# The first attention block begins with its own four units, and layer 0's last tokens begin at the second unit

## The chip, the cores and the metric

The kernel runs on one core of a Trainium2 chip. The core has five engines that take their instructions in order and wait for each other through semaphores: TensorE (PE in the profile; its weight loads are PEld), VectorE (DVE), ScalarE (ACT), GpSimd (POOL) and SyncE (SP), whose queue issues most DMA transfers. The metric is the device time of one execution in microseconds (us), lower is better. The change is judged by the median of several runs.

## The reference

Four images of 128 channels and 64 x 64 pixels go through two layers. Layer 0 normalises by groups of channels, makes three 1x1 convolutions and attends over the 4096 pixels; its result is added to the input. Layer 1 takes the pixels as tokens of 128 channels: an attention of 16 heads with 8 channels each, a small feed-forward part, and a recurrence over the tokens. The change lies in layer 1's attention, cut here to what matters.

```python
def _L1_attn_ref(x, rx_theta, ...):
    heads = x.reshape(Bs, Ss, H, D)                 # H = 16 heads, D = 8
    qkv = _qz_ring(heads + rx_theta)                # products of cosines
    q = jnp.transpose(qkv, (0, 2, 1, 3))
    scores = jnp.einsum('bhsd,bhtd->bhst', q, q) / np.sqrt(D)
    attn = jax.nn.softmax(scores, axis=-1)
    ctx = jnp.einsum('bhst,bhtd->bhsd', attn, q)
    ...
```

Queries, keys and values are the same `q`. The matrix of scores is therefore symmetric, and the kernel computes only about half of it: the exponentials of a tile serve its rows, and, transposed, its columns.

## The kernel before

**Stages.** An image n goes through `first_stage` (layer 0, and its tokens in 8 chunks of 512), `second_stage` (layer 1's attention) and later, between the steps of the next image, its feed-forward part. The tokens of a chunk are made by the generator `tokens` (line 674), in some 15 steps between `yield`s: statistics (line 717), `normalise` (721), the cosines in `cos_steps` (224), products (746 to 751), a transposition (759) and two transfers into `parts_dram` (767). The last chunk is not finished in layer 0: its generator is handed to `attention` (line 769) as `tail`, and one step of it runs in each unit there (line 1198), from the third unit on. When it has ended, `rest` (853) loads the last quarter of keys and queries. Until then no unit may use tokens of the last quarter (line 1118).

**Units.** The 16 heads are taken as 8 pairs. For a pair the 4096 queries are cut into 4 blocks (`NQB`) of 1024 (`QB`), and the keys into 32 tiles of 128. A unit is one turn of the loop at line 1117: two tiles of keys against the block's queries. Its work:

- TensorE: scores into PSUM (line 1125, four matmuls in four parts of the array).
- ScalarE: two exponentials of 128 x 1024 (line 1137). Their place is chosen by `exps` (1089): a pool of six tiles, or, in two of five turns, parts of the image's tile `xs`, which layer 0 no longer needs (while `tail` lives, only the first of the two).
- TensorE, two units later: `weigh` (929) adds the weighted values into `acc`, a PSUM tile with one buffer (`ps_acc=(ONE, 1)`), new in each block.
- When a block's last unit has been weighed, `finish` (968) has VectorE transpose `acc` into `o` (line 972), GpSimd copy `o` (980), and later steps gather the rest.

**Own units and the others.** The order of a block's units comes from `order` (1066). Four of them are the block's own: both tiles lie in the block's own 1024 tokens, and nothing of them serves another block (`off` is false at line 1120). The other units, `off`, serve a second block too: ScalarE also sums their exponentials (`accum_out`), VectorE transposes them ("flips", line 900, in `run_flips`), and TensorE then makes mirror steps (line 913): a group of four off units gives 16 steps, each of four matmuls. They add up in one of two slots of the PSUM tile `misc`, and VectorE adds the sum into `later` (927). Blocks 0 and 1 of a pair have 16 off units and 4 own ones, blocks 2 and 3 have 12 and 4. In most blocks the own units stand between the others, one after each four (each three); only in the very last block of an image they come last.

**What sets the order.** The engines' order around attention is written out by hand (`tc.manual_schedule`, line 1747): TensorE, ScalarE, VectorE and GpSimd take instructions as the Python code issues them. SP's transfers are placed by the scheduler. Three rules meter the mirror work:

- A unit adds to `credit` 3.3 steps (3.15 from block 2 on) if it is off, and 3.0 if it is own, up to 4.75 and 8.25 (lines 1150 to 1156). `run_pending` (875) takes that many whole steps, of one group only. A group is available two turns after its fourth flip (line 902).
- `run_flips` (891) issues the flips of at most two units a turn (line 1196).
- It holds the flips of a group while the group two before it has steps left, because a group's flipped tiles are used again:

```python
                if g >= 2 and groups[g - 2]["steps"]:
                    return
```

**Loads.** `prepare` (807) asks for a pair's keys and queries, one tile for each block, from pools of six tiles each. In pair 0 the first loads are those that the first unit needs (lines 845 to 850); the last block's wait for `rest`. The scratch tiles of `tail` come from the same pools.

Of the kernel before, what the change touches and what calls it, by code (L numbers as in the profile page):

```python
# [26 lines left out]
def kernel(  # L27
# [42 lines left out]
    NQB = S // QB  # L70
# [41 lines left out]
    def get(kind, name):  # L112
        if callable(here[kind]):
            return here[kind](name)
        pool, shape = here[kind]
        return pool.tile(shape, F32, tag=kind, name=name)
# [652 lines left out]
    def attention(n, q, xs, tail, upcoming):  # L769
# [12 lines left out]
        fixed, _ = here["fixed"]  # L782
# [24 lines left out]
        def prepare(pair):  # L807

            own = qb[:, :, ts(pair, 2 * D)].rearrange("p (k a) (h d) -> p a k h d", a=4, d=D)
            qa = q_aug[pair % 2]  # L810
            qv = qa[:, 0 : NT * 2 * V].rearrange("p (k s h e) -> p s k h e", s=4, h=2, e=V)

            def copy_q(k0, k1):
                for a in range(4):
                    for s in range(4):
                        nc.gpsimd.tensor_copy(  # L816
                            qv[ts(a, 32), s, k0:k1, :, 0:D], own[ts(s, 32), a, k0:k1]
                        )

            keys = [get("keys", f"keys{n}_{pair}_{b}") for b in range(NQB)]
            queries = [get("queries", f"queries{n}_{pair}_{b}") for b in range(NQB)]
            def load_queries(b):
                for h in range(2):
                    for x in range(2):
                        for y in range(2):
                            row = ((2 * pair + h) * 2 + y) * D
                            src = parts_dram[row : row + D, ts(2 * b + x, IC)]
                            nc.sync.dma_start(  # L830
                                out=queries[b][ds(64 * h + 32 * x + 16 * y, 16), :],
                                in_=src.unsqueeze(0).broadcast_to([2, D, IC]),
                            )

            def load_keys(b):
                for h in range(2):
                    row = (2 * pair + h) * 2 * D
                    src = parts_dram[row : row + 2 * D, ts(b, QB)]
                    nc.sync.dma_start(
                        out=keys[b][ts(h, 64), :], in_=src.unsqueeze(0).broadcast_to([4, 2 * D, QB])  # L840
                    )


            there = NQB if pair else NQB - 1
            load_keys(1)
            load_queries(0)
            for b in [0] + list(range(2, there)):
                load_keys(b)
            for b in range(1, there):
                load_queries(b)  # L850
            copy_q(0, NTG if pair else NTG - 1)

            def rest():
                if pair == 0:
                    copy_q(NTG - 1, NTG)
                    load_keys(NQB - 1)
                    load_queries(NQB - 1)

            later = get("later", f"later{n}_{pair}")
            nc.gpsimd.memset(later, 0.0)  # L860
            denom = get("denom", f"denom{n}_{pair}")
            return (keys, queries, qa, later, denom), rest
# [28 lines left out]
        def run_flips(most):  # L891
            while most and flips:
                g, k, es = flips[0]
                if g >= 2 and groups[g - 2]["steps"]:
                    return
                group = groups[g]
                if k == 0:
                    group["e"] = [get("flipped", f"t{group['name']}_{h}") for h in range(2)]
                for h in range(2):
                    nc.vector.transpose(group["e"][h][:, k, :], es[h])  # L900
                if k == TG - 1:
                    pending.append((turn + 2, group["steps"], group["block"]))
                flips.pop(0)
                most -= 1
# [158 lines left out]
            else:  # L1063
                late.extend([mirrored, result])

        def order(b, own_last):


            own = [(QT * b + k, QT * b + TG + k) for k in range(TG)]
            halves = [(v, v) for v in range(2 * b + 2, 2 * b + (5 if b < NQB // 2 else 4))]  # L1070
            halves.insert(2, (2 * b + 1, 2 * b + (5 if b < NQB // 2 else 4)))
            rest = [
                tuple(v % (2 * NQB) * TG + k for v in vs) for vs in halves for k in range(TG)
            ]
            if own_last:
                return rest + own
            each = len(rest) // TG
            return [u for k in range(TG) for u in rest[each * k : each * (k + 1)] + own[k : k + 1]]

# [9 lines left out]
        def exps(name, last):  # L1089


            k = turn % 5 - 3
            if k < 0 or last or (k and tail):
                return [get("exps", f"e{name}_{h}") for h in range(2)]
            return [xs[:, ts(2 * k + h, QB)] for h in range(2)]

        waiting = []
        turn = 0
# [4 lines left out]
        ends, late = [], []  # L1103
        fixed_tiles()
        ready, rest = prepare(0)
        w = mirror_weights(0, 0)
        for pair in range(NPAIR):
            keys, queries, qa, later, denom = ready
            for b in range(NQB):
                block = {"acc": None}  # L1110
                end_of_all = pair == NPAIR - 1 and b == NQB - 1
                tiles = order(b, end_of_all)

                coming = (pair, b + 1) if b < NQB - 1 else (pair + 1, 0)
                if coming[0] == NPAIR:
                    coming = None
                for at, unit in enumerate(tiles):
# [4 lines left out]
                    for h in range(2):  # L1122
                        for x in range(2):
# [6 lines left out]
                                stop=True,  # L1130
                            )
                    es = exps(name, end_of_all)

                    split = off and unit[0] != unit[1]
# [38 lines left out]
                    if at == 6 and b == 1 and pair + 1 < NPAIR:  # L1173
                        upcoming_pair = prepare(pair + 1)[0]
# [20 lines left out]

                    if at:
                        run_flips(2)
                    if tail and turn > 2 and next(tail, tail) is tail:
                        tail = None
                        rest()  # L1200
                    if end_of_all and at in (0, len(tiles) - 1):
# [509 lines left out]
    def second_stage(im, tail, upcoming):  # L1711
# [33 lines left out]
        with stage(f"attn{n}", sides, others, ("queries", "keys"), **pools):  # L1745
            engines = {e.engine for e in (nc.tensor, nc.scalar, nc.vector, nc.gpsimd)}
            with tc.manual_schedule(engines=engines):
                im["left"] = attention(n, im["q"], im["xs"], tail, upcoming)
# [109 lines left out]
    for n in range(N):  # L1858
# [5 lines left out]
        tail = first_stage(image, before)  # L1864
# [153 lines left out]
    with tc.If(any_bad > 0):  # L2018
# [5 lines left out]
        with stage(  # L2024
# [8 lines left out]
            pool, _ = here["big"]  # L2033
# [95 lines left out]
```

## Time and profile before

| | us |
|---|---|
| median of 3 runs | 6939.8 (6939.42 to 6941.01) |
| the profiled execution, its own time | 6941.1 |
| its span, first to last instruction | 6939.0 |
| mean granted TensorE clock | 0.992 |
| attention of image 0: first scores, first scores of pair 1, of pair 2, of pair 3 | 397.8, 560.7, 715.0, 869.3 |
| the same of image 1 | 2096.7, 2258.5, 2412.8, 2567.1 |
| the same of image 2 | 3794.8, 3955.2, 4109.6, 4263.9 |
| the same of image 3 | 5494.2, 5654.8, 5809.1, 5963.4 |
| half clock of TensorE in image 0's first block | 400.9 to 407.7, and 428.2 to 431.6 |
| in image 1's | 2100.7 to 2107.6, and 2124.6 to 2131.4 |
| in image 2's | 3797.2 to 3804.0, and 3824.5 to 3827.9 |
| in image 3's | 5497.0 to 5503.8, and 5524.3 to 5527.7 |

The first part of the profile's page lists each engine's busy time, its share of the span and its instructions. Later rows are groups of instructions: line, engine, operation, what is written and read, count, busy time, mean duration in ns, and idle time of the engine just before them, with what ended it. In a timeline a row begins with its start and length in us. A wait is put down to the instruction that ended it. The granted clock is a share of full speed; outside the stretches above it is 1.0 in the attention of pairs 0 to 3.

### The profile page before, as it was taken

Reading aid. Unit: us, or ns where it says so; the run is one execution under the profiler, and the core shown is the slowest. Engines: PE = TensorE matmul, PEld = TensorE weight load, DVE = VectorE, ACT = ScalarE, POOL = GpSimd, SP = SyncE. Lnnn points to the kernel's source line nnn. Section 1 sums busy time; section 2 is a strip of 40 time slices with the busy share of each in tenths; the row PEclk is TensorE's granted clock in tenths of the full one; section 3 lists DMA queues with packets and bytes.
Section 4 is the critical chain, followed back from the end, with each engine's and each line's share of the span. In section 5 each row is a group of like instructions: output and inputs, shape, how many; then the busy total and the mean of one; then the engine's idle time right before and its main releaser. Section 6 shows DMA issues by size and latency. Waiting matters only on the chain. (4 is left out here: it accounts for less than half of the span.)

```text
span 6939.0 us, 223539 instructions
## 1 busy us (share of the span) xinstructions
PE 6806.3 (98%) x92343; PEld 3652.9 (53%) x92343; DVE 5971.1 (86%) x8073; ACT 5931.6 (85%) x11841; POOL 2775.2 (40%) x10008
## 2 busy tenths in 40 slices
PE   9999999999999999999999999999999999999997
PEld 5545555555664555555565455555566555555554
DVE  6688988897888899889788999888978898889888
ACT  4479999997668999999676999999956699999985
POOL 1134444444333444444433344444443343444443
PEclk9999999999999999999999999999999999999998
DMA  1110000000111000000011100000001100000013
GB/s 33 40 39 30 27 31 21 22 10 23 46 53 44 31 24 25 21 22 9 31 50 52 40 25 24 25 21 24 18 28 49 51 31 21 22 24 24 20 54 119
DMA packets 88792, 226.17 MB, mean 33 GB/s; under 512 B 9832, under 2 KB 10736, under 8 KB 86992
## 3 DMA queue, kind: packets, MB, share of 16 engines
q1 hardware_dynamic: 85772, 206.39, 8.8%
q8 instruction: 726, 11.89, 0.7%
q10 hardware_dynamic: 1732, 5.24, 0.2%
q14 instruction: 306, 2.51, 0.1%
q0 software_dynamic: 256, 0.13, 0.0%
HBM read 147.73 MB, written 56.62 MB: 29 GB/s over the span
## 5 line engine op out<-in xcount | busy, mean ns | idle before, releaser
L1137 ACT ACTIVATE e<-s 128x1024 f32<-128x1024 f32 (+1 forms) x3480 | 2949.8, 902 | 94.0 <-PE s L1125 71.5
L900 DVE STREAM_TRANSPOSE t<-e 128x1024 f32<-128x1024 f32 x2240 | 2593.4, 1210 | 63.2 <-ACT e L1137 60.2
L913 PEld LDWEIGHTS misc<-t,mirror 128*32 128x32 f32 x57344 | 1654.8, 110 | 1327.8 <-issue 1278.8
L913 PE MATMUL misc<-t,mirror 128*32 128x128 f32 x57344 | 1967.6, 273 | 20.2 <-DVE later L927 14.3
L1137 ACT ACTIVATE xs<-s 128x1024 f32<-128x1024 f32 (+1 forms) x2152 | 1838.7, 908 | 58.8 <-PE s L1125 46.1
L900 DVE STREAM_TRANSPOSE t<-xs 128x1024 f32<-128x1024 f32 x1344 | 1562.6, 1210 | 37.7 <-ACT xs L1137 36.2
L934 PE MATMUL acc<-e,q_aug 128*32 128x512 f32 x11360 | 1522.7, 608 | 1.2 <-POOL q_aug L816 1.2
L1125 PE MATMUL s<-queries,keys 32*128 32x512 f32 x9216 | 1240.4, 496 | 9.6 <-ACT e L1137 5.7
L980 POOL COPY own<-o 32x36 f32<-32x36 f32 x2048 | 432.2, 211 | 1838.4 <-DVE o L972 1758.5
L934 PE MATMUL acc<-xs,q_aug 128*32 128x512 f32 x7072 | 942.2, 605 | 0.0
L573 ACT ACTIVATE p<-s 128x1024 f32<-128x1024 f32 x512 | 500.4, 1022 | 412.3 <-PE s L569 408.2
L1125 PEld LDWEIGHTS s<-queries,keys 32*128 32x128 f32 x9216 | 485.4, 182 | 587.3 <-issue 293.3
L580 PE MATMUL acc<-p,asmT 128*128 128x512 f32 x1536 | 707.7, 595 | 0.0
L1137 ACT ACTIVATION_READ_ACCUMULATOR e<-s 128x1 f32 x2880 | 696.0, 242 | 0.0
L1005 POOL COPY other<-turned 32x64 f32<-32x64 f32 x1904 | 444.4, 233 | 620.2 <-DVE turned L995 541.7
L870 POOL COPY mirror<-q 32x128 f32<-32x128 f32 x2048 | 596.2, 291 | 188.7 <-PE misc L913 100.6
L594 DVE TENSOR_TENSOR total<-total,p 128x1024 f32<-128x1024 f32 x448 | 548.4, 1224 | 23.5 <-ACT p L573 15.6
L569 PE MATMUL s<-hl,e 128*128 128x512 f32 x1536 | 442.1, 429 | 5.7 <-ACT p L573 4.7
L580 PEld LDWEIGHTS acc<-p,asmT 128*128 128x128 f32 x1536 | 287.8, 190 | 262.0 <-issue 245.2
L966 POOL COPY by_token<-by_key 32x4 f32<-32x4 f32 x2000 | 387.6, 194 | 84.4
L1137 ACT ACTIVATION_READ_ACCUMULATOR xs<-s 128x1 f32 x1728 | 420.7, 243 | 0.0
L934 PEld LDWEIGHTS acc<-e,q_aug 128*32 128x32 f32 x11360 | 225.5, 108 | 351.8 <-issue 349.9
(355 smaller groups left out, 5066.8 us busy)
## 6 DMA issues: line engine op xcount, KB each, us to landing
keys<-parts_dram SPq DMA_DIRECT2D x256, 256.0 KB
queries<-parts_dram SPq DMA_DIRECT2D x1024, 32.0 KB
x_dram<-x SPq DMA_DIRECT2D x56, 256.0 KB
fx<-x_dram SPq DMA_DIRECT2D x48, 256.0 KB
t_dram<-t2T SPq DMA_DIRECT2D x32, 256.0 KB
t2s<-t_dram SPq DMA_DIRECT2D x16, 512.0 KB
hl<-hl SPq DMA_DIRECT2D x28, 256.0 KB
parts_dram<-high SPq DMA_DIRECT2D x28, 256.0 KB
```

The lines of the kernel that those rows point to most:

```text
L569: nc.tensor.matmul(s[:, j, :], stationary, moving, start=y == 0, stop=y == len(parts) - 1)
L573: nc.scalar.activation(p, s, AF.Exp)
L580: nc.tensor.matmul(state["acc", ic], values_at(tile_of(2 * jp + j)), p[:, j, :], start=jp == 0 and j == 0, stop=jp == NP - 1 and j == 1,)
L594: nc.vector.tensor_tensor(state[ic], state[ic], p, ALU.add)
L870: nc.gpsimd.tensor_copy(wv[ts(a, 32), s, :, :, ts(a, D)], own[ts(s, 32)])
L900: nc.vector.transpose(group["e"][h][:, k, :], es[h])
L913: nc.tensor.matmul(state["acc"][ts(2 * x + h, 32), :], state["w"][:, QT * (s // 4) + TG * x + s % 4, h, :], state["e"][h][:, :, ds(IC * x ...
L934: nc.tensor.matmul(it["in"]["acc"][ts(2 * h + x, 32), :], it["qa"][:, ds((2 * it["tiles"][x] + h) * V, 32)], it["e"][h][:, ts(x, IC)], sta ...
L980: nc.gpsimd.tensor_copy(own[ts(s, 32), ts(x, 4), h, :], ov[ts(2 * h + x, 32), s, :, 0:V])
L1005: copy(to[ts(k, 32), h], tv[ts(2 * x + h, 32), k])
L1125: nc.tensor.matmul(ss[h][:, x, :], keys[unit[x] // QT].bitcast(F32R)[r, ts(unit[x] % QT, P)], queries[b].bitcast(F32R)[r, :], start=True, ...
L1137: nc.scalar.activation(es[h][:, ts(x, IC)] if split else es[h], ss[h][:, x, :] if split else ss[h].rearrange("p x c -> p (x c)"), AF.Exp, ...
```

## The change

Four edits, all in `attention`:

1. `order` gets an argument `own_first`. In block 0 of pair 0 of each image the four own units come first, and then the other 16 without interruption.
2. `tail` begins at the second unit (`turn > 1`) and no longer at the third.
3. In pair 0 the tile of keys of block 1 is taken from the pool ahead of that of block 0, and the keys of block 0 are loaded first, since the first unit now reads them.
4. While `tail` lives, `exps` doesn't use `xs` in the first five turns.

```diff
-            keys = [get("keys", f"keys{n}_{pair}_{b}") for b in range(NQB)]
+            keys = {b: get("keys", f"keys{n}_{pair}_{b}") for b in ((0, 1, 2, 3) if pair else (1, 0, 2, 3))}
...
-            load_keys(1)
+            load_keys(1 if pair else 0)
             load_queries(0)
-            for b in [0] + list(range(2, there)):
+            for b in [0 if pair else 1] + list(range(2, there)):
                 load_keys(b)
...
-        def order(b, own_last):
+        def order(b, own_last, own_first):
...
-            if own_last:
-                return rest + own
+            if own_last or own_first:
+                return own + rest if own_first else rest + own
...
-            if k < 0 or last or (k and tail):
+            if k < 0 or last or (tail and (k or turn < 5)):
                 return [get("exps", f"e{name}_{h}") for h in range(2)]
...
-                tiles = order(b, end_of_all)
+                tiles = order(b, end_of_all, pair == b == 0)
...
-                    if tail and turn > 2 and next(tail, tail) is tail:
+                    if tail and turn > 1 and next(tail, tail) is tail:
                         tail = None
                         rest()
```

The computation, the number of instructions on each engine and the rules for `credit`, `run_flips` and `run_pending` are the same. The lines of the two kernels have the same numbers.

## The prediction

> **What bounds the kernel now.** I read the page first, then TensorE's and VectorE's timelines around the first attention block, the windows with the granted clock, and last the view of line 972, because the change delays the work that surrounds it.
>
> ```profile
> PE 6806.3 (98%) x92343; PEld 3652.9 (53%) x92343; DVE 5971.1 (86%) x8073; ACT 5931.6 (85%) x11841; POOL 2775.2 (40%) x10008
> ...
> L900 DVE STREAM_TRANSPOSE t<-e 128x1024 f32<-128x1024 f32 x2240 | 2593.4, 1210 | 63.2 <-ACT e L1137 60.2
> ```
> TensorE is busy 98% of the span; VectorE has 14% spare over the whole, and a flip (line 900) is its costliest work.
>
> ```profile
> 453.80 0.50 PE L1125 MATMUL s<-queries,keys 32*128 32x512 f32 x4
> 454.24 1.06 PE L934 MATMUL acc<-e,q_aug 128*32 128x512 f32 x8
> 455.12 1.06 PE L913 MATMUL misc<-t,mirror 128*32 128x128 f32 x32
> 456.11 0.50 PE L1125 MATMUL s<-queries,keys 32*128 32x512 f32 x4
> ```
> One unit on TensorE, by distances between starts: scores 0.44, weighing 0.88, four mirror steps 0.99 (0.25 each). A unit lasts 2.31 us with four steps, 2.08 with three.
>
> ```profile
> 422.69 1.06 PE L934 MATMUL acc<-e,q_aug 128*32 128x512 f32 x8
> 427.94 1.75 PE L913 MATMUL misc<-t,mirror 128*32 128x128 f32 x32 [4.19 <-DVE later L927]
> ...
> 422.00:428.00 6.00, 1.81 (x28) 0.46 (x24) 6.00 (x8) 5.50 (x16) 0.00 (x0) 1.00 0.00 0
> 428.00:432.00 4.00, 4.00 (x52) 2.09 (x56) 4.00 (x4) 1.77 (x3) 2.43 (x6) 0.57 0.00 0
> 450.00:470.00 20.00, 20.00 (x352) 10.14 (x352) 17.47 (x19) 19.24 (x36) 13.53 (x49) 1.00 0.24 90
> ```
> (The last three lines: stretch, length, busy time of TensorE, its weight loads, VectorE, ScalarE, GpSimd, each with its instructions, granted clock, DMA share, GB/s.) Image 0, 25 us into attention: VectorE, full with flips and layer 0's last tokens (6.00 of 6), is late; TensorE waits 4.19 us and then works at 0.57 of its clock. The four images' such waits sum to 14.3 us. From 450 on TensorE never stops.
>
> ```profile
> L972 DVE STREAM_TRANSPOSE o<-acc x128: 707/717/718, 453.1 to 6739.3; 128x512 f32<-128x512 f32 x128
> ...
>   PE acc L934: 132.3, 125
> who waited for it (us, times):
>   POOL own L980: 1758.5, 100
>   PEld acc L934: 0.3, 1
> ```
> At the end of a block VectorE transposes the sum `acc` out of its only PSUM buffer. 125 times of 128 VectorE sat waiting for TensorE; TensorE waited for it once, 0.3 us. This margin is what the change spends.
>
> **Own units first: the mirror work starts four units later.** An own unit makes no flip and no mirror step. Counted from 0, units 0 to 3 were off-diagonal; their group of 16 steps was released two turns after the fourth, at unit 6. Now units 4 to 7 are the first group, and its steps begin at unit 10. Steps run in the pattern 4, 4, 3, 3, 2 a group, so by the end of the 20-unit block the old order has done 46 of 64 (units 6 to 19), the new one 32 (units 10 to 19): 14 steps behind. No work is added, but catching up is slow. The credits pay 3.3 steps an off unit (3.15 from block 2 on) and 3.0 an own: 64.8 in blocks 0 and 1, 49.8 in blocks 2 and 3, against 64 and 48 needed, a surplus of 2(0.8 + 1.8) = 5.2 a pair. 14 / 5.2 = 2.7 pairs.
>
> **Where the lag bites.** Line 894 holds the flips of group g until group g-2 has no steps left. In the old block 0, group (8,8) has its last step in unit 10, just as the first unit two groups on asks for its flip: nothing is held. In the new one that last step falls in unit 14, and the asking units are 12 to 15. From block 1 on a whole group is held and then released in two turns: 8 transposes back to back. By VectorE's rows six starts cover 6.8 us, so 1.13 each and 9.0 for eight, in some 4.2 us of TensorE's time.
>
> I replayed both built orders with this trace's numbers: each engine takes its instructions in order, one starts when its engine's slot is over and what it waits for has ended; slots are median distances between starts. The old order, replayed, puts pair 3 469 to 471 us after each image's attention start; the trace has 471.5, 470.4, 469.1 and 469.2. So I trust the replay inside attention to a few us an image.
>
> One stall, worked out. Pair 0, unit 54: group g-2 ends and eight flips start, with line 972 behind them: 9.0 + 0.72 = 9.7 us until `acc` is free. TensorE asks for the new block's `acc` at unit 58, after three units (6.2) and one set of scores (0.5): 6.7 us. It stands 3.0 us; the replay says 3.1. Queued behind that weighing are the mirror steps that would free the next flips, and all later scores. The trace of before shows no such wait beyond 0.3 us. Bounds for one: 0 (VectorE's spare time takes it) and 7.1 (release one turn ahead: 9.7 less 2.6). For the block ends of the lag the replay gives 0.4, 3.1, 2.8, 3.6, 2.7, 0.7, 1.3, 1.5, 0.7: 17 us an image, nearer the lower end, and I take it.
>
> **The sum.** TensorE's idle time in the first four pairs, old to new in the replay: 10 to 31 us in image 0, 8 to 24 in the others: +70 in all. This already contains what the change cures: in images 1 to 3 the old wait of 3.2 to 3.5 us shrinks to 0.7 and block 1 begins some 3 us earlier. In image 0 it is not cured: GpSimd still copies mirror weights (line 870) until 410, so the tail's reciprocal root (line 221, ended at 411.2) comes no earlier, normalising stands on it, and behind that now every flip; the held exps stop ScalarE.
>
> Next, 57 more sets of scores begin in halves, since the second half waits for an exp that waits for a late flip. The four matmuls of a set overlap, and a split costs up to another 0.43: at most 24, the replay has 21.
>
> Last, the clock. The old trace grants half clock after stretches that were 0.4 to 0.7 busy; image 1's wait of 3.2 us cost 6.8 us of it. The replay, halving below 0.58 busy, has 61 us more at half clock: 31 us lost. Halving below 0.50 gives 22, below 0.66 53. I take 31, since 0.58 lies between what the trace shows.
>
> The Trainium skill ("TensorE: Matmul & The Clock Gate", Part 1) says that TensorE falls to half clock only after an idle window of about 3.4 us; by that rule hardly a stall of 2.7 to 3.6 us would cool it, and the sum would be some 91 instead of 122. The trace's 3.2 us wait did cool it, so I keep the row.
>
> 70 + 21 + 31 = 122. The profiled execution took 6941.1 (span 6939.0 and 2.1 around it), 1.3 above the median 6939.8, which lies between runs of 6939.42 and 6941.01; so 6939.8 + 122 = **about 7062 us, slower by 1.8%.** I say 7060.
>
> **The edits costed at nothing.** Starting the tail one turn earlier puts VectorE's tokens ahead of the flips (inside the replay). Unit 3's exps move from `xs` to the pool: its six tiles hold three units, and unit 0's are free once weighed, since nothing flips them. Keys: block 0's and block 1's halves are issued tens of us before attention in both orders; without that cover the first scores would wait a landing, of which the nearest row is 1.84 us for a 256 KB write. On SP's queue nine of pair 1's query loads (three before) now pass the last keys of pair 0, and the ninth waits for block 0's queries until unit 19. Those keys are wanted at unit 30, eleven units or 23 us later; without that cover TensorE would stand some 2 us an image. GpSimd's queue keeps its order, but the next block's mirror copies now wait for a lagging group (5.3 us of copies, a 42 us block to hide in).
>
> **Rivals.** *The start is cured and the lag is free* (VectorE's spare time absorbs the bursts; for it: 426 us busy of 473 in the first three pairs of image 1, against it: bursts do not wait for an average). Then the 14.3 us of waits go and about half of 17 us at half clock, 8.5; four more units without steps, idle 0.7 us each (2.0 for two exps by ScalarE's starts, 400.76 and 401.75, less 1.3), give back 11 over four images: 6939.8 - 23 + 11, about 6928. Chance 0.04. *A wash*: the lag catches up within pair 0, so only the first three or so of the waits arise, some 3 us an image after the gain of 3: 6935 to 6952. Chance 0.03. *The lag is worse*: each of the four long stalls costs two windows of half clock as image 1's did, and ScalarE starves for free exps: half-clock cost 53 or more, 7085 to 7120. Chance 0.13. *No effect*, since the order would be rebuilt by a scheduler: against it, the built order shows own units first on TensorE, ScalarE and VectorE.
>
> **How the numbers follow.** Forecast 0.80: 7060, its own range 7025 to 7085. The range of 8 in 10 takes in part of the worse case and a replay that counts half of the idle time: 7020 to 7095. A change under 0.2% (14 us) could not be told from none; faster 0.04, same 0.03, slower 0.93.
>
> **What would show it.** Right: in the changed profile line 934 on TensorE waits for line 972, some nine times over 0.3 us an image, all in pairs 0 to 2; half clock then; pairs 3 to 7 as long as before; the wait on line 927 gone in images 1 to 3. Wrong: no wait on line 972, or pair 3 beginning within 5 us of its old distance from the start (I expect 25 to 37 more). If the first block of images 1 to 3 is not about 3 us shorter, the start was misread.

## The result, and the profile after

| | before | after |
|---|---|---|
| median of 5 runs beside each other, us | 6941.01 (6939.42 to 6944.32) | 7066.35 (7063.72 to 7066.51) |
| span of the profiled execution | 6939.0 | 7064.6 |
| TensorE busy | 6806.3 | 6856.1 |
| TensorE at half clock, all stretches added | 120.1 | 167.5 |

The changed kernel is slower: ratio 1.018, 95% interval 1.0169 to 1.0191. The forecast was 7060, in a range from 7020 to 7095.

The first part of the page of after, and four of its rows (the columns are those of before):

```profile
PE 6856.1 (97%) x92343; PEld 3678.3 (52%) x92343; DVE 5965.9 (84%) x8073; ACT 5947.4 (84%) x11841; POOL 2774.2 (39%) x10008
...
L900 DVE STREAM_TRANSPOSE t<-e 128x1024 f32<-128x1024 f32 x2240 | 2588.6, 1208 | 43.2 <-ACT e L1137 41.2
L913 PE MATMUL misc<-t,mirror 128*32 128x128 f32 x57344 | 1984.3, 274 | 10.6 <-DVE t L900 5.8
...
L934 PE MATMUL acc<-e,q_aug 128*32 128x512 f32 x11392 | 1535.4, 611 | 53.4 <-DVE o L972 52.1
...
L934 PE MATMUL acc<-xs,q_aug 128*32 128x512 f32 x7040 | 942.3, 607 | 19.8 <-DVE o L972 19.8
```

Every engine has as many instructions as before, and a flip costs the same 1.21 us. The new thing stands at the end of the two rows of line 934: 52.1 and 19.8 us of idle time, ended by line 972. Before, the same two rows had 1.2 and 0.0 us of idle time, none of it from line 972:

```profile
L934 PE MATMUL acc<-e,q_aug 128*32 128x512 f32 x11360 | 1522.7, 608 | 1.2 <-POOL q_aug L816 1.2
...
L934 PE MATMUL acc<-xs,q_aug 128*32 128x512 f32 x7072 | 942.2, 605 | 0.0
```

TensorE's waits in after, longest sums first (what waited, for what: us in all, times, longest one):

```profile
PE acc L934 <- DVE o L972: 71.9, 36, 3.7
PE s L1125 <- ACT e L1137: 18.3, 30, 1.7
...
PE misc L913 <- DVE t L900: 5.8, 5, 3.3
```

Before, the second of these was 5.7 us in 12 waits, and another one stood there, which is gone:

```profile
PE misc L913 <- DVE later L927: 14.3, 4, 4.2
```

Line 972 itself, in the view that lists who waited for it:

```profile
  PE acc L934: 79.8, 75
...
who waited for it (us, times):
...
  PEld acc L934: 90.9, 60
  PE acc L934: 71.9, 36
```

The first line is VectorE's side: it now sat waiting for TensorE 75 times, where it had done so 125 times of 128. The last line is TensorE's side: 36 waits, 2.0 us each, nine in each of the four images, where before there was one of 0.3 us that held only the weight load.

One of them at close range, the first weighing of block 3 of pair 0 in image 0. First VectorE's timeline in after:

```profile
532.43 4.62 DVE L900 STREAM_TRANSPOSE t<-e 128x1024 f32<-128x1024 f32 x4
536.97 4.58 DVE L900 STREAM_TRANSPOSE t<-xs 128x1024 f32<-128x1024 f32 x4
541.47 0.67 DVE L972 STREAM_TRANSPOSE o<-acc 128x512 f32<-128x512 f32 x1
```

and TensorE's timeline beside it:

```profile
538.60 0.50 PE L1125 MATMUL s<-queries,keys 32*128 32x512 f32 x4
542.20 1.06 PE L934 MATMUL acc<-e,q_aug 128*32 128x512 f32 x8 [3.10 <-DVE o L972]
543.09 1.12 PE L913 MATMUL misc<-t,mirror 128*32 128x128 f32 x24
544.14 0.80 PE L1125 MATMUL s<-queries,keys 32*128 32x512 f32 x4
```

Eight flips run back to back from 532.43 to 541.55 and the small transposition of `acc` stands behind them, 0.67 us long. TensorE has nothing left at 539.10 and waits until 542.20. From 543.5 on its instructions are longer (a set of scores 0.80 instead of 0.50). That is the clock, as the windows of the same stretch show (stretch, length, busy time and instructions of TensorE, granted clock, DMA share, GB/s):

```profile
536.66:540.07 3.41, 2.44 (x40) 1.00 0.26 84
540.07:543.49 3.42, 1.29 (x24) 1.00 0.15 57
543.49:546.90 3.41, 3.41 (x36) 0.50 0.11 43
```

The wait of 3.10 us is followed by 3.41 us at half clock: some 1.7 us more are lost.

### The profile page after: what moved, and what is told of

Same layout as the page of the kernel before. It is cut to its first block, busy times and chain, and to the rows that moved or that the text cites. A ratio compares the mean times of both kernels' runs of the same rounds, so it can differ in the third digit from the quotient of the medians.

```text
span 7064.6 us, 223521 instructions
## 1 busy us (share of the span) xinstructions
PE 6856.1 (97%) x92343; PEld 3678.3 (52%) x92343; DVE 5965.9 (84%) x8073; ACT 5947.4 (84%) x11841; POOL 2774.2 (39%) x10008
## 5 line engine op out<-in xcount | busy, mean ns | idle before, releaser
L934 PE MATMUL acc<-e,q_aug 128*32 128x512 f32 x11392 | 1535.4, 611 | 53.4 <-DVE o L972 52.1
L900 DVE STREAM_TRANSPOSE t<-xs 128x1024 f32<-128x1024 f32 x1344 | 1558.9, 1208 | 16.6 <-ACT xs L1137 15.1
L1125 PE MATMUL s<-queries,keys 32*128 32x512 f32 x9216 | 1268.7, 498 | 24.4 <-ACT e L1137 18.3
L934 PE MATMUL acc<-xs,q_aug 128*32 128x512 f32 x7040 | 942.3, 607 | 19.8 <-DVE o L972 19.8
L1125 PEld LDWEIGHTS s<-queries,keys 32*128 32x128 f32 x9216 | 500.8, 182 | 585.7 <-issue 320.1
L1137 ACT ACTIVATION_READ_ACCUMULATOR e<-s 128x1 f32 x2880 | 680.4, 236 | 0.0
L927 DVE TENSOR_TENSOR later<-later,misc 128x128 f32<-128x128 f32 (+1 forms) x576 | 162.1, 281 | 460.1 <-PE misc L913 456.0
```

Source lines behind the costliest of these rows:

```text
L934: nc.tensor.matmul(it["in"]["acc"][ts(2 * h + x, 32), :], it["qa"][:, ds((2 * it["tiles"][x] + h) * V, 32)], it["e"][h][:, ts(x, IC)], sta ...
L1125: nc.tensor.matmul(ss[h][:, x, :], keys[unit[x] // QT].bitcast(F32R)[r, ts(unit[x] % QT, P)], queries[b].bitcast(F32R)[r, :], start=True, ...
L1137: nc.scalar.activation(es[h][:, ts(x, IC)] if split else es[h], ss[h][:, x, :] if split else ss[h].rearrange("p x c -> p (x c)"), AF.Exp, ...
```

## The experiments

All changes of time are against runs of the kernel before, taken on the same chip beside those of the changed one. The waits are those of the matmuls, from the profiled execution; waits of a weight load alone aren't counted. "Shift of pair 3" is by how much later than before pair 3 begins, counted from the image's attention start, summed over the four images. Half clock is TensorE's time at half clock, in the whole profiled execution and in pairs 0 to 2 of the four images (before: 120.1 and 44.4). Outside these pairs it varies from 62 to 99 us with no visible relation to the waits, so the column of pairs 0 to 2 is the one to compare.

| kernel | time, us | ratio (95%) | change | waits of line 934 for 972 | half clock | of it in pairs 0 to 2 | shift of pair 3 |
|---|---|---|---|---|---|---|---|
| after | 7066.35 | 1.0169 to 1.0191 | +125 | 71.9 | 167.5 | 88.7 | +128 |
| order_alone | 7078.55 | 1.0176 to 1.0210 | +133 | 72.1 | 174.6 | 99.0 | +134 |
| rest_alone | 6943.64 | 0.9987 to 1.0006 | -2 | none | 146.9 | 47.8 | +1 |
| old_late_steps | 7084.29 | 1.0183 to 1.0217 | +139 | 70.0 | 188.2 | 116.1 | +148 |
| catch_up | 6954.28 | 1.0004 to 1.0023 | +9 | none | 119.5 | 37.5 | +13 |
| one_own_first | 6947.99 | 0.9998 to 1.0016 | +5 | none | 130.1 | 44.4 | +6 |
| two_own_first | 6951.07 | 1.0003 to 1.0022 | +8 | 6.6 | 133.2 | 44.4 | +8 |
| three_own_first | 7001.79 | 1.0075 to 1.0108 | +59 | 43.3 | 133.5 | 71.7 | +62 |
| two_own_faster_start | 6951.69 | 1.0003 to 1.0021 | +9 | 5.3 | 125.0 | 47.8 | +7 |
| acc_copied | 7006.57 | 1.0077 to 1.0111 | +64 | copy instead | 121.6 | 37.5 | +61 |
| acc_copied_old | 7008.92 | 1.0079 to 1.0113 | +66 | copy instead | 124.9 | 41.0 | +54 |

The kernel before had medians of 6945.32, 6942.88 and 6942.89 beside the three groups of experiments. The last column agrees with the change of time to within 12 us everywhere: what a kernel loses, it loses in the first three pairs of each image.

### Which of the four edits it is

**order_alone**: the kernel before with the first edit only.

```diff
-                tiles = order(b, end_of_all)
+                tiles = order(b, end_of_all, pair == b == 0)
...
+            if own_last or own_first:
+                return own + rest if own_first else rest + own
```

> The old kernel with the own units first in block 0 of pair 0 and nothing else of the change (tail from the third unit, keys, queries and exps as before). Lag theory: the order alone makes the mirror steps late, so nearly all of the cost is here: +110 to +140 us over before, line 934 waits for line 972 some 36 times, 60 to 75 us in sum. Rival 'the moved tail, the exchanged keys or the exps edit cost the time': within 15 us of before.

Measured +133, with the same waits as after. From TensorE's waits of this kernel:

```profile
PE acc L934 <- DVE o L972: 72.1, 37, 3.7
```

**rest_alone**: the other three edits on the old order.

```diff
-                tiles = order(b, end_of_all)
+                tiles = order(b, end_of_all, False)
...
-            if k < 0 or last or (k and tail):
+            if k < 0 or last or (tail and (k or turn < 5)):
...
-                    if tail and turn > 2 and next(tail, tail) is tail:
+                    if tail and turn > 1 and next(tail, tail) is tail:
```

> The changed kernel with the old order of units, so the other three edits alone. Lag theory: no lag, no wait on line 972; -10 to +5 us against before, with the 14 us of waits on line 927 nearly as before. Rival 'the other edits cost it': +60 us or more.

Measured no change (-2), and the old wait of line 913 for line 927 is still there, 12.8 us in all. So the order of the units carries the whole loss. The other edits cost nothing by themselves. With the new order it is +125 with them and +133 without, but the intervals of the two ratios overlap, so that they take some of its cost away isn't shown.

### Whether it is the lag of the mirror steps

**old_late_steps**: the kernel before with its old order, where only the first group's steps are released four turns later. No unit moves.

```diff
-                    pending.append((turn + 2, group["steps"], group["block"]))
+                    pending.append((turn + (6 if g == 0 else 2), group["steps"], group["block"]))
```

> The old kernel and the old order of units; only the first group of 16 mirror steps of each image is released six units after its last flip and not two, which makes the same lag of four units without any other order. Lag theory: +110 to +150 us, waits of line 934 on line 972 of 55 to 75 us, all in pairs 0 to 2. Rival 'sixteen off-diagonal units in a row overload VectorE and ScalarE in the first block': the order is the old one, so at most the four units' missing steps, 0 to +15 us.

Measured +139. This is the clearest of the runs: the order of the units is the old one, and the lag alone brings the waits and the loss. From TensorE's waits of this kernel:

```profile
PE acc L934 <- DVE o L972: 70.0, 33, 3.7
PE s L1125 <- ACT e L1137: 35.0, 38, 3.2
```

**catch_up**: the changed kernel, with the credit of blocks 0 and 1 of pair 0 raised to 4.0 steps a unit.

```diff
+                    if pair == 0 and b < 2:
+                        rates = (4.0, 4.0)
```

> The changed kernel, with credits of 4.0 steps a unit in blocks 0 and 1 of pair 0 (before 3.3 and 3.0), so that the 14 steps of lag are paid back within the first 40 units. Lag theory: +5 to +25 us over before in place of +125; waits on line 972 under 10 us in sum; pair 1 begins 0 to 8 us later than before, counted from the attention's start. Rival 'sixteen units in a row': no better than the changed kernel, or worse since a unit then lasts longer. Rival 'half clock at the start is the cost': unchanged.

Measured +9. Line 972 is no longer among the waits of TensorE's matmuls, and all the added half clock is gone (37.5 us in pairs 0 to 2 against 44.4 before). The new order is kept and costs little, once the lag is made good within two blocks. Half of what is left sits in image 0: there pair 3 still begins 6.3 us later than before, in the other images 1.4 to 2.6.

### How much lag it takes

**one_own_first, two_own_first, three_own_first**: the changed kernel, with only the first one, two or three own units ahead of the block; the others stand between the groups as before (the diff shows one; `n_own` is 2 and 3 in the other two).

```diff
-                return own + rest if own_first else rest + own
+                if own_first:
+                    n_own = 1
+                    out = list(own[:n_own])
+                    for g in range(4):
+                        out += rest[4 * g : 4 * g + 4]
+                        out += own[n_own:][g : g + 1]
+                    return out
+                return rest + own
```

> The changed kernel, but only two own units stand first, and the other two after the first and the second four off-diagonal units. The lag is two units, some 7 steps. Lag theory with its threshold (flips are held only when the last step of the group two before falls after the asking unit, and the old order has about no room): a few held flips, waits on line 972 of 3 to 15 us in sum, -5 to +20 us against before. Rival 'each own unit moved to the front costs the same': half of the change's 125, +60.

> The same with three own units first, the fourth after the first four off-diagonal ones. Lag of three units, some 10 steps, paid back in about two pairs. Lag theory: waits on line 972 of 30 to 50 us in sum, +45 to +85 us. Rival 'each own unit costs the same': +94.

> The changed kernel with one own unit ahead of block 0 and the other three between the groups. Theory (waits begin only past a threshold of lag; two own units first gave 6.6 us of waits on line 972 and +8, three gave 43.3 and +59): one own unit first leaves TensorE under 3 us of waits on line 972 in all, half clock within 120 to 135 us, and a time from 8 below to 3 above the kernel before: within what can't be told from no change. Rival (every unit of lag costs its share, some 15 us of time a unit): +10 to +20.

Measured +5, +8, +59, and +125 with all four; the waits are none, 6.6, 43.3 and 71.9 us. The first two units of lag are almost free, the third costs some 51 us (the four runs with three spread over 13 us) and the fourth some 66. So there is a threshold, as the worked stall of the prediction would have it: as long as VectorE reaches line 972 before TensorE has used up its three units, nobody waits. The size of that margin, three units, was not varied. one_own_first came out 2 us above what was expected of it. Its interval holds 1, so it isn't told from no change.

**two_own_faster_start**: two own units first, with 3.55 steps a unit in blocks 0 and 1 of pair 0 (the lines of catch_up, with another number). It was meant to take the last waits away.

> Two own units first, the rest of the own units between the groups, and blocks 0 and 1 of pair 0 paid at 3.55 steps a unit, which makes good the lag of two units within those blocks. Theory (the remaining 6.6 us of waits of two own units first are lag): the waits on line 972 fall under 3 us and the time is 8 below to 3 above the kernel before. Rival (the +8 of two own units first comes from image 0's later start and from VectorE's tail, not from lag): it stays at +5 to +12.

The theory missed and the rival fits: the waits only fell from 6.6 to 5.3, and the time stayed at +9. Of its 7 us of shift 4.8 lie in image 0. No version that was run beats the kernel before by more than can be told from no change.

### Whether the wait on line 972 is the price, or only stands beside it

**acc_copied** has ScalarE copy `acc` to SBUF first, in pairs 0 to 2, so that TensorE can go on before VectorE's transposition. **acc_copied_old** does the same in the kernel before, since the copy has a price of its own.

```diff
-            nc.vector.transpose(o, block["acc"])
+            if pair < 3:
+                raw = half_tile(f"raw{n}_{pair}_{b}")
+                nc.scalar.copy(raw, block["acc"])
+                nc.vector.transpose(o, raw)
+            else:
+                nc.vector.transpose(o, block["acc"])
...
-            queries=((P, IC), 6),
+            queries=((P, IC), 5),
...
-            half=(HALF, 1),
+            half=(HALF, 2),
```

(A scratch use of layer 0 was moved to other tiles to make room: `third(0, "xh0", "xh1")`.)

> The changed kernel with its lag and its held flips as they are, but in pairs 0 to 2 ScalarE copies acc to SBUF at a block's end (about 0.6 us, 12 times an image) and VectorE transposes the copy, so that the PSUM buffer doesn't wait for VectorE's queue. To make room, one buffer of queries less, and two scratch tiles of the next image's opening are shared. Lag theory with line 972 as its main price: the 72 us of waits on it and most of the added half clock go, some 17 us of waits for the copy come: +25 to +60 us over before. Rival 'the price is paid elsewhere (exps that wait for flips, half clock from the start)': still +90 or more.

> The same copy of acc in the old kernel, as the measure of what the copy itself costs: +30 to +60 us over before (TensorE waits for ScalarE's copy at each of the 48 block ends, and line 927's add comes later). So the changed kernel with the copy should stand within 20 us of the old one with the copy, where without it they stand 125 apart.

Both came out slightly slower than expected, +64 and +66. But the two are now 2.4 us apart, where without the copy the two orders are 125 apart. The same place as above, in acc_copied, on VectorE:

```profile
531.69 4.62 DVE L900 STREAM_TRANSPOSE t<-e 128x1024 f32<-128x1024 f32 x4
536.23 4.58 DVE L900 STREAM_TRANSPOSE t<-xs 128x1024 f32<-128x1024 f32 x4
540.74 0.67 DVE L975 STREAM_TRANSPOSE o<-raw 128x512 f32<-128x512 f32 x1
```

and on TensorE:

```profile
539.03 1.07 PE L934 MATMUL acc<-e,q_aug 128*32 128x512 f32 x8 [0.71 <-ACT raw L974]
```

The eight flips are as long as in after, and the transposition comes as late, at 540.74. But TensorE waits 0.71 us for the copy instead of 3.10 for the transposition, and it keeps its full clock. So the waits on line 972 and the half clock behind them come from the only buffer of `acc` being drained by an instruction queued behind the burst: with another way to drain it both are gone (37.5 us at half clock in pairs 0 to 2), though the flips come as before.

The lag isn't free for all that. The sets of scores that begin in halves, the prediction's second term, stay with it, and no run takes that term away by itself: in pairs 0 to 2, 136 of the 864 sets have their first and fourth matmul more than 0.2 us apart, as many as in after, where before and acc_copied_old have 92. Nor is the copy a cure. In both kernels TensorE waits for it 48 times, and in acc_copied_old the old wait of line 913 for line 927, 14.3 us before, grows. The first row below is of acc_copied, the other two of acc_copied_old:

```profile
PE acc L934 <- ACT raw L974: 29.3, 48, 1.1
...
PE misc L913 <- DVE later L927: 38.3, 28, 4.1
PE acc L934 <- ACT raw L974: 29.2, 48, 0.7
```

So the two kernels pay much the same for unlike reasons, acc_copied for the copy and for its split sets, acc_copied_old for the copy and for line 927, and that they end only 2.4 us apart is partly chance. Some 13 of the 66 us of acc_copied_old stay unexplained by these waits.

## Why the prediction was right

**The lag and its end.** Right. With the lag alone the old order loses as much as the new one, and with the lag paid back the new order loses 9. Pair 3 was to begin 25 to 37 us later, and began 36.3, 30.4, 31.2 and 29.7 later. From pair 3 to pair 7 the shift no longer grows (36.1 at pair 7 in image 0, 30.1 in image 1).

**The waits on line 972.** Right, one by one. The nine in image 0 were 0.50, 3.10, 2.91, 3.73, 2.80, 0.73, 1.77, 1.64 and 0.82 us; the other images agree to 0.05. The forecast's nine sum to 17 an image, 68 in four; measured 71.9. That VectorE has spare time on average did not help: 16% of the span is spare in after, and yet 36 waits arise.

**The three terms of the sum.** The total was nearly met (122 forecast; 125.6 by the two spans), the terms less well. They were measured in the two traces in pairs 0 to 2, where the shift is 127.7 us.

| term | before, us | after, us | lost | forecast |
|---|---|---|---|---|
| TensorE idle | 25.5 | 102.4 | 77 | 70 |
| at half clock, of which half is lost | 44.4 | 88.7 | 22 | 31 |
| first to fourth start of a set of scores, all sets added | 47.6 | 92.7 | 30 | 21 |

In the last row, 15.1 of the 45.1 us added is idle time, which the first row has already, so 30.0 remain. The split sets were undersized: 44 more sets are split by over 0.2 us (28 more if pairs 3 to 7 are counted too; 57 forecast), but the splits lose more than the 24 that the forecast called the most. The clock was oversized; the last section shows where the replay's bound of 0.58 goes wrong. The three measured terms make 129. So the idle time was forecast 7 too low, the clock 9 too high and the sets 9 too low; these errors partly cancel, and that the total came within 4 us is luck to that extent. Taken in the same way from the trace of each other kernel, the three terms add up to its shift of pair 3 to within 7 us. The last term is over some 3 us only in the four kernels with the whole lag (29 to 35) and in catch_up (13).

**The start of images 1 to 3.** The mechanism was right, the size too large. The wait on line 927 did go, and with it the half clock 28 to 30 us into the images (3.4 to 6.8 us each). But block 1 begins only 2.0, 0.9 and 2.0 us earlier, not 3. Nor is this a gain: 14 mirror steps are still owed by then, 14 x 0.25 = 3.5 us of TensorE's work. In catch_up, which pays most of them at once, block 1 begins 49.3 to 49.4 us after the start, where it was 50.7, 49.4 and 49.5 before.

**Image 0 is not cured.** Right. TensorE's timeline there in after:

```profile
425.91 0.41 PE L913 MATMUL misc<-t,mirror 128*32 128x128 f32 x4 [3.31 <-DVE t L900]
426.94 1.48 PE L913 MATMUL misc<-t,mirror 128*32 128x128 f32 x28 [0.62 <-DVE t L900]
428.35 0.80 PE L1125 MATMUL s<-queries,keys 32*128 32x512 f32 x4
```

The wait of 4.19 us before is now 3.31 + 0.62, for a flip instead of line 927, again followed by half clock. Block 1 begins 2.4 us later than before and block 2 5.9. That GpSimd's copies (line 870) hold the tail up there was read from the trace; it was not tried by a run.

**The edits costed at nothing** cost nothing: rest_alone.

**The rivals.** The cured start with a free lag fails on both counts, since the start gave 2 us at most and the idle time grew by 75.8. The wash is what one_own_first and two_own_first do; four units are past the threshold. In the worse case each long stall was to cost two windows of half clock. In image 0 each cost one; in images 2 and 3 the longest cost two, and the last none. No effect is excluded by the interval.

**The rule on the clock.** The Trainium skill ("TensorE: Matmul & The Clock Gate", Part 1) lets the clock fall only after about 3.4 us of idleness. Here waits of 2.80 to 3.12 us were enough, as the row of before (3.2 us) had said, and in one place even one of 1.77. The sum by that rule, 91, lies 35 below the measured 125.6.

## What to carry to other kernels

Before moving work that another engine feeds, look at what stands behind it in that engine's queue: a burst that the average hides still delays every short instruction behind it, and if one of these frees a buffer that exists once, the bottleneck engine stops. The margin can be read before the change (how often the draining instruction sat waiting for its input, 125 times of 128 here), and it holds up to a threshold: two units of lag cost 8 us here, four 125. A late start of a metered stream needs a faster rate right after it, as in catch_up; a surplus of a few per cent carries the lag through several pairs.

## What the hardware showed that was not expected

The same wait cools TensorE in one image and not in another. The wait of 2.80 us (the first weighing of block 2 of pair 1) was followed by half clock in images 0 and 1, and by none in images 2 and 3. Two windows of after, in image 1 and in image 2 (stretch, length, busy time of TensorE, its weight loads, VectorE, ScalarE, GpSimd, clock, DMA share, GB/s):

```profile
2407.20:2410.60 3.40, 0.61 (x11) 0.29 (x12) 3.19 (x4) 2.61 (x6) 0.15 (x1) 1.00 0.07 28
2410.60:2414.00 3.40, 3.40 (x36) 1.58 (x29) 0.00 (x0) 0.00 (x0) 2.81 (x15) 0.50 0.00 0
...
4134.30:4137.70 3.40, 2.57 (x44) 1.21 (x40) 3.40 (x4) 3.40 (x7) 0.00 (x0) 1.00 0.15 50
4137.70:4141.10 3.40, 1.44 (x29) 0.84 (x32) 1.91 (x3) 1.32 (x4) 1.22 (x6) 1.00 0.01 3
4141.10:4144.50 3.40, 3.40 (x52) 1.32 (x47) 1.13 (x3) 2.58 (x3) 2.12 (x11) 1.00 0.00 0
```

Half clock begins and ends on a grid: in image 0 at 543.5, 584.5, 632.2, 680.0 and 751.7, which lie 12, 14, 14 and 21 times 3.41 us apart. In image 1 the wait (2407.66 to 2410.45) falls into one cell of that grid, in image 2 (4136.86 to 4139.66) it is shared by two. Near the middle the share of a cell alone doesn't decide, though: in image 2 a cell with 1.44 us busy of 3.40 was followed by full clock, while in image 0 one with 1.63 of 3.40 (748.30 to 751.70, holding a wait of 1.77) was followed by half:

```profile
748.30:751.70 3.40, 1.63 (x36) 1.00 0.26 105
751.70:755.10 3.40, 3.40 (x40) 0.50 0.21 81
```

(Stretch, length, busy time of TensorE, clock, DMA share, GB/s.) What else counts was not tried.

How wide that middle is can be counted. In the twelve profiled executions of this document, each cut along its own grid, the busy share of TensorE in a cell and the clock of the next cell go together like this (cells at full clock only):

| busy share of the cell | cells | followed by half clock |
|---|---|---|
| under 0.40 | 186 | 184 (the other two begin 2 us into an execution) |
| 0.40 to 0.65 | 294 | 95 |
| over 0.65 | 23605 | 1 |

The replay of the prediction halved below 0.58, in the middle of the open range, where most cells kept full clock. Its "0.4 to 0.7 busy" was read from stretches beside the grid: cut along it, the cells ahead of the half clock at the attention starts of before were 0.08 to 0.70 busy.

The Trainium skill ("TensorE: Matmul & The Clock Gate", Part 1) says that the activity window is free-running, which the grid agrees with; that a window has to be idle as a whole, as its table reads, the windows above contradict (0.61 us busy, then half clock).
